# Query projections as seven products of halves, score tiles in banks of their own, block transfers over three queues

## The chip, the cores and the metric

The kernel runs on one core of a Trainium2 chip. The metric is the device time of one execution in microseconds. The kernel before took 1106.41 us, the median of three runs (1105.07 to 1107.13).

## The reference, cut to what matters

All data are float32. There are 1024 rows of width 512, 32 query heads and 8 key and value heads of width 128, so that a group of four query heads shares one key and value head.

```python
def attn(x, w_q, w_k, w_v, w_o):                # x: (1, 1024, 512), w_q: (512, 4096)
    q = (x @ w_q).reshape(B, S, Hkv, g, D)      # Hkv = 8 groups, g = 4 heads, D = 128
    k = (x @ w_k).reshape(B, S, Hkv, D)
    v = (x @ w_v).reshape(B, S, Hkv, D)
    scores = einsum("bqhgd,bkhd->bhgqk", q, k) * D ** -0.5
    scores = where(causal, scores, -inf)
    return einsum("bhgqk,bkhd->bqhgd", softmax(scores), v).reshape(B, S, -1) @ w_o

x = x + layernorm(attn(layernorm(x), w_q, w_k, w_v, w_o))
x = x + layernorm(ffn(layernorm(x)))            # a linear layer plus routed low-rank experts
```

The feed-forward part at the end is not touched by the change.

## The kernel before

The 1024 rows are 8 tiles of 128, t = 0 to 7. A *block* is one group of heads g and one tile t of queries, and there are 64. A *pair* is two tiles of one group, 256 queries (u = 0 to 3). Lines 86 to 88 fix the order: groups 0 to 5 one after the other, four pairs each, and then groups 6 and 7 in turn, pair by pair, with u = 0, 3, 2, 1. In the loop from line 798 on, block i brings together the scores of block i, the attention-weighted values of block i - 2 (line 803), the output projection of a pair finished earlier (line 808, even i), the query projection of the next pair (lines 687 to 694, odd i) and the key and value projections that fall due (lines 695 to 713). The pieces stand in a list `then`, and `run_share` deals it out: a quarter of its columns after each of the four steps of scores. The query pieces stand ahead of the rest.

**Query projection** (`project_q`, line 337). It makes the transposed queries of 4 heads x 256 rows. The contraction of 512 is four chunks of 128, so a pair takes 16 matmuls of 256 columns, a float32 matmul being two records in the trace. Two heads share a PSUM bank, and `nc.scalar.mul` (line 350) scales them and writes them to qT. The group's weights are two tiles, `wq0` for heads 0 and 1 and `wq1` for heads 2 and 3, loaded by ScalarE's queue for a new group (line 722) in its predecessor's block t = 6.

**Scores** (`scores`, line 404). A block has four steps j. A step takes 32 queries of each of the 4 heads, 128 rows, against all keys up to n = 128 t + 32 (j + 1): one or two matmuls of at most 512 columns. VectorE adds the mask (line 426) and takes the maximum (428), Pool writes zeroes into the rest of p (431), ScalarE takes the exponential and its sum (433). A step later VectorE takes the reciprocal (439), ScalarE scales p (440), and VectorE transposes p in 32 x 32 pieces into T (446). The score tile is two banks, and two of them exist. Where t is below 4, a score fits into one bank, and the step of an odd j takes the second bank of the tile of the step before it (lines 410 to 414).

**Block transfers** (`to_keys`, line 458). After the last step of a block, 16 DMAs bring T into the layout K that the values' matmuls read, queries becoming columns. Blocks 3 to 62 issue all of them on SP's queue; the first three and the last issue in turn on SP, SP and Pool (lines 452 to 454). T and K have one buffer for even and one for odd t.

**Banks.** PSUM has eight: four in the two score tiles, one for the weighted values (`bank_pv`), three for all else (`bank`).

**Order on the engines.** Matmuls, transposes, DMAs and the instructions under `keep` stay in the order of the program. The framework may place the others, the Pool's sums of weights among them, and adds semaphores where data demand them. VectorE, ScalarE and Pool each work through their queue in order. Pool also holds `combine_o` (line 500), four subtractions per group for an output projection that is already made of seven products of halves (`project_o_pair`, line 514).

Of the kernel before, what the change touches and what calls it, by code (L numbers as in the profile page):

```python
# [22 lines left out]
def kernel(  # L23
# [28 lines left out]

    nc = tc.nc
    S, H = x.shape
    D = P
# [30 lines left out]
    blocks = [(g, 2 * u + e) for g, u in pairs for e in range(2)]  # L88
    N = len(blocks)
    N2 = (G - 2) * NT  # L90

    def keep(ins):
        return tc.keep_in_program_order(ins)
# [26 lines left out]
    def load_q(g, i, by=nc.scalar):  # L120

        if weights.get(("q", i), (None,))[0] == g:
            return
        hw = R * D // 2
        w = wp.tile([P, KC, hw], F32, tag=f"wq{i}", name=f"wq_{g}_{i}", bufs=1)
        load(w, w_q[:, ts(2 * g + i, hw)].rearrange("(c p) n -> p c n", p=P), by)
        weights["q", i] = (g, w)

    def load_v(gv, i, by=nc.scalar):

# [111 lines left out]
    def bank(name):  # L242
        return ps_m.tile([P, 512], F32, tag="pm", name=name)
# [81 lines left out]
    def project_k(g, qb):  # L325
        def finish(pm):
            kT = kTs[g, qb] = act.tile([P, QB], F32, tag="kT", name=f"kT_{g}_{qb}", bufs=2 * NQB)
            nc.scalar.copy(kT, pm)

        def term(c):  # L330
            return weights["k", g][:, c, :], xnT[qb][:, c, :]

        return chained(
            lambda: bank(f"pk_{g}_{qb}"), [lambda c=c: term(c) for c in range(KC)], finish
        )

    def project_q(g, u):

        pm = {}

        def get(j):
            if j % 2 == 0:
                pm[0] = bank(f"pq_{g}_{u}_{j}")
            return pm[0][:, ts(j % 2, PQ)]

        def finish(j):
            if j == 0:
                qTs[g, u] = act.tile([P, PQ // SQ, R, SQ], F32, tag="qT", name=f"qT_{g}_{u}")
            if j % 2:
                nc.scalar.mul(  # L350
                    qTs[g, u][:, :, j - 1 : j + 1, :].rearrange("p s h q -> p h s q"),
                    pm[0].rearrange("p (h s q) -> p h s q", h=2, q=SQ),
                    scale,
                )

        def term(j, c):
            w = weights["q", j // 2]
            assert w[0] == g
            rhs = xnT[u * PQ // QB][:, c, ts(u % (QB // PQ), PQ)]
            return w[1][:, c, ts(j % 2, D)], rhs  # L360

        work = []
        for j in range(R):
            terms = [lambda j=j, c=c: term(j, c) for c in range(KC)]
            if j == 0:
                ends = lambda pm: finish(0)
            else:
                ends = lambda pm, j=j: finish(j)
            work += chained(lambda j=j: get(j), terms, ends, PQ)
        return work  # L370

    turned, keyed = {}, {}

# [30 lines left out]
    def scores(g, t, j):  # L404

        n = t * P + (j + 1) * SQ
        full = (t + 1) * P
        name = f"{g}_{t}_{j}"

        if t < TPB and j % 2:  # L410
            s = score_tile.pop(0)[:, QB:]
        else:
            s = ps_s.tile([P, S], F32, tag="s", name=f"s_{name}")
            score_tile[0] = s
        for c0 in range(0, n, QB):
            w = min(QB, n - c0)
            matmul(
                s[:, c0 : c0 + w],
                qTs[g, t // 2][:, (t % 2) * NSUB + j, :, :].rearrange("p h q -> p (h q)"),
                kTs[g, c0 // QB][:, :w],  # L420
                start=True,
                stop=True,
            )
        pin = keep if blocks.index((g, t)) >= N2 + 2 else lambda ins: ins
        rescale_scores()
        keep(nc.vector.tensor_tensor(s[:, n - SQ : n], s[:, n - SQ : n], smask, ALU.add))  # L426
        nmax = small.tile([P, 1], F32, tag="nmax", name=f"nmax_{name}")
        keep(nc.vector.tensor_reduce(nmax, s[:, :n], AX.X, ALU.max, negate=True))  # L428
        p = act.tile([P, S], F32, tag="p", name=f"p_{name}", bufs=3)
        if n < full:  # L430
            nc.gpsimd.memset(p[:, n:full], 0.0)  # L431
        total = small.tile([P, 1], F32, tag="total", name=f"total_{name}")
        keep(nc.scalar.activation(p[:, :n], s[:, :n], AF.Exp, bias=nmax, accum_out=total))  # L433
        finish_scores()
        work_off(1 + len(deferred) // 5)

        def rescale():
            rec = small.tile([P, 1], F32, tag="rec", name=f"rec_{name}")
            keep(nc.vector.reciprocal(rec, total))  # L439
            keep(nc.scalar.mul(p[:, :n], p[:, :n], rec))  # L440

        def finish():
            if j == 0:
                turned[g, t] = turn_view(turn_tile("T", g, t), t)
            pin(
                nc.vector.transpose(  # L446
                    turned[g, t][:, :, j, :, :].rearrange("p b k q -> p k b q"),
                    p[:, :full].rearrange("p (k b q) -> p k b q", b=R, q=SQ),
                )
            )  # L450
            if j == NSUB - 1:
                three = (nc.sync, nc.sync, nc.gpsimd)
                alone = 3 <= blocks.index((g, t)) < N - 1
                to_keys(g, t, by=three[:1] if alone else three)

        score_tile["rescale"], score_tile["finish"] = rescale, finish

    def to_keys(g, t, by=(nc.sync,)):

        src = turned.pop((g, t))  # L460
        dst = keyed[g, t] = turn_view(turn_tile("K", g, t), t)
        for h in range(R):
            for b in range(NSUB):
                load(dst[ts(b, SQ), h], src[ts(h, SQ), b], by[(h * NSUB + b) % len(by)])
# [217 lines left out]
    def projections(i):  # L682
# [5 lines left out]
        if i == 0:  # L688
            later["q"] = project_q(*pairs[m])
            q = later["q"][: 2 * KC]  # L690
        elif i == 1:
            q = later["q"][2 * KC :]
        elif i % 2 and m < len(pairs):
            q = project_q(*pairs[m])
        if i < N2:
            if t == 2:
                other += project_k(g, 1)
# [56 lines left out]
    def weave(a, b):  # L754

        na, nb = sum(c for c, _ in a), sum(c for c, _ in b)
        merged, at, bt, b = [], 0, 0, list(b)
        for c, f in a:
            merged.append((c, f))
            at += c  # L760
            while b and (bt + b[0][0] / 2) * na <= at * nb:
                bt += b[0][0]
                merged.append(b.pop(0))
        return merged + b
# [33 lines left out]
    for i in range(N):  # L798
# [13 lines left out]
            begins = ffn_router(t)  # L812

        rest = o + weave(o_pair, other + pv[:2] + begins[1:] + pv[2:])
        then = begins[:1] + q + ends[:-1] + rest[:4] + ends[-1:] + rest[4:]
        for n in range(NSUB):
            scores(*blocks[i], n)
            run_share(then, n, NSUB)
        if i == 1:
            combine_o(0)  # L820
        if i == NT:
# [68 lines left out]
```

## Time and profile before

| what | us |
|---|---|
| median of 3 runs | 1106.41 |
| the profiled execution's own time | 1105.28 |
| its span | 1103.5 |
| TensorE busy | 1074.5 |
| VectorE busy | 654.0 |
| ScalarE busy | 491.2 |
| Pool busy | 113.8 |
| query projections, 1024 matmul records | 235.7 |
| scores, 768 matmul records | 273.8 |
| weighted values, 576 matmul records | 277.3 |

A line of the profile that describes a group of instructions has the source line, the engine and operation, the tile written and the tiles read, the shape and the count, then the busy time in us, the mean duration of one in ns, and the engine's idle time ahead of it with what ended that. A line of waits has the engine and line that waited, what it waited for, the total in us, the number of waits and the longest. A row of stretches has, for each engine, the busy time and the number of instructions, then TensorE's granted clock and the share and rate of the DMA engines. The durations of single matmuls overlap, so the distance between their starts tells their cost, not the duration.

### The profile page before, as it was taken

How to read it: one execution, taken by the hardware profiler on the slowest of the kernel's cores; microseconds unless marked ns; L12 is line 12 of the kernel's file. 1: busy time of each engine (PE TensorE's matmuls, PEld its weight loads, DVE VectorE, ACT ScalarE, POOL GpSimd, SP SyncE). 2: the span in 40 equal slices, each digit the busy share in tenths (PEclk: the TensorE clock that was granted, in tenths of full speed). 3: DMA queues.
4: the chain of work that ended last, by engine and by line, in shares of the span. 5: the costliest groups of instructions: out<-in, count | busy, mean ns of one | idle time of the engine just before them, and what ended most of it. 6: DMA issues, size and time to landing. Idle time of an engine off the chain costs nothing.

```text
span 1103.5 us, 12827 instructions
## 1 busy us (share of the span) xinstructions
PE 1074.5 (97%) x3836; PEld 704.5 (64%) x3836; DVE 654.0 (59%) x1529; ACT 491.2 (45%) x991; POOL 113.8 (10%) x299
## 2 busy tenths in 40 slices
PE   8899999999999999999999999999999999999895
PEld 6676666666776666656676666666777556466452
DVE  4466555765465545766456654765446766566746
ACT  2554534554354434554354443555335554453501
POOL 2400012000020002000020000100020110111212
PEclk9999999999999999999999999999999999999998
DMA  5145342455125431454224441365333655444221
GB/s 181 40 107 141 67 115 58 125 144 115 24 68 155 107 82 45 113 144 105 52 60 125 121 104 37 93 176 123 86 102 100 166 144 116 127 107 104 68 67 38
DMA packets 79061, 111.82 MB, mean 101 GB/s; under 512 B 18176, under 2 KB 50560, under 8 KB 78992
## 3 DMA queue, kind: packets, MB, share of 16 engines
q1 hardware_dynamic: 52976, 82.08, 31.5%
q10 hardware_dynamic: 25040, 27.27, 7.9%
q0 software_dynamic: 976, 1.65, 0.6%
q8 instruction: 31, 0.51, 0.2%
q14 instruction: 38, 0.31, 0.1%
HBM read 33.34 MB, written 2.10 MB: 32 GB/s over the span
## 4 chain that ended last, share of the span: by engine, by line
PE 82%; DVE 7%; ACT 5%; DMA 2%; issue 1%; SPq 1%; POOL 1%; ACTq 0%; POOLq 0%; DVEq 0%
PE po L100 20%; PE s L100 18%; PE pq L100 16%; PE pk L100 4%; PE pv L100 4%; PE pe L100 4%; PE pa L100 3%; ACT p L433 2%; PE pO L100 2%; PE pc L100 2%; PE pb L100 2%; PE pd L100 2%; DVE T L446 2%; PE pf L100 2%; DVE nmax L428 2%; ACT p L440 2%
## 5 line engine op out<-in xcount | busy, mean ns | idle before, releaser
L100 PE MATMUL s<-kT,qT 128*128 128x512 f32 (+15 forms) x768 | 273.8, 465 | 8.7 <-ACT p L433 8.6
L100 PE MATMUL po<-K,v 128*128 128x512 f32 x576 | 277.3, 596 | 4.3 <-DMA K<-T 2.6
L433 ACT ACTIVATE p<-s,nmax 128x32 f32<-128x32 f32 (+31 forms) x256 | 179.2, 700 | 203.1 <-DVE nmax L428 197.9
L440 ACT ACTIVATE p<-p,rec 128x32 f32<-128x32 f32 (+31 forms) x256 | 187.9, 734 | 179.3 <-DVE rec L439 121.0
L446 DVE STREAM_TRANSPOSE T<-p 128x128 f32<-128x128 f32 (+7 forms) x256 | 198.2, 775 | 100.4 <-ACT p L440 89.4
L100 PE MATMUL pq<-xnT,wq 128*128 128x256 f32 x1024 | 235.7, 379 | 0.0
L100 PEld LDWEIGHTS s<-kT,qT 128*128 128x128 f32 x768 | 144.0, 190 | 137.4 <-issue 105.5
L100 PEld LDWEIGHTS pq<-xnT,wq 128*128 128x128 f32 x1024 | 192.8, 190 | 38.5 <-issue 16.5
L428 DVE TENSOR_REDUCE nmax<-s 128x1 f32<-128x32 f32 (+31 forms) x256 | 180.6, 705 | 8.2
L100 PEld LDWEIGHTS po<-K,v 128*128 128x128 f32 x576 | 107.8, 191 | 78.0 <-issue 63.3
L426 DVE TENSOR_TENSOR s<-s,smask 128x32 f32<-128x32 f32 x256 | 47.8, 187 | 132.2 <-PE s L100 131.5
L431 POOL MEMSET p<- 128x96 f32 (+2 forms) x192 | 29.7, 155 | 848.4 <-DVE T L446 782.9
L439 DVE RECIPROCAL rec<-total 128x1 f32<-128x1 f32 x256 | 39.8, 155 | 55.1 <-ACT p L433 53.2
L100 PE MATMUL pv<-wv,xnT 128*128 128x256 f32 x256 | 69.1, 388 | 0.9 <-ACT xnT L264 0.9
L350 ACT ACTIVATE qT<-pq 128x512 f32<-128x512 f32 x64 | 38.1, 595 | 71.1 <-PE pq L100 71.1
L474 ACT COPY attnT<-po 128x512 f32<-128x512 f32 x64 | 37.4, 584 | 63.2 <-PE po L100 63.0
L100 PE MATMUL pk<-xnT,wk 128*128 128x512 f32 x128 | 64.5, 593 | 0.0
L100 PE MATMUL pa<-wo,attnT 128*128 128x256 f32 x224 | 62.7, 390 | 0.0
L100 PEld LDWEIGHTS pv<-wv,xnT 128*128 128x128 f32 x256 | 49.1, 194 | 11.0 <-issue 2.7
L100 PEld LDWEIGHTS pa<-wo,attnT 128*128 128x128 f32 x224 | 41.6, 192 | 19.4 <-issue 14.5
L433 ACT ACTIVATION_READ_ACCUMULATOR p<-s,nmax 128x1 f32 x256 | 49.5, 193 | 0.0
L523 DVE TENSOR_TENSOR sums<-attnT 128x256 f32<-128x256 f32 x28 | 11.9, 425 | 56.8 <-ACT attnT L474 56.7
(120 smaller groups left out, 776.6 us busy)
## 6 DMA issues: line engine op xcount, KB each, us to landing
K<-T SPq DMA_DIRECT2D x128, 128.0 KB, 2.4
K<-T SPq DMA_DIRECT2D x128, 112.0 KB, 2.2
wq<-in_w_q_dram ACTq DMA_DIRECT2D x27, 512.0 KB, 4.8
K<-T SPq DMA_DIRECT2D x128, 96.0 KB, 2.2
K<-T SPq DMA_DIRECT2D x128, 80.0 KB, 2.1
K<-T SPq DMA_DIRECT2D x123, 64.0 KB, 2.0
wo<-in_w_o_dram ACTq DMA_DIRECT2D x28, 256.0 KB, 3.8
K<-T SPq DMA_DIRECT2D x123, 48.0 KB, 1.9
```

What stands on the lines that cost most here:

```text
L100: keep(nc.tensor.matmul(*args, **kw))
L350: nc.scalar.mul(qTs[g, u][:, :, j - 1 : j + 1, :].rearrange("p s h q -> p h s q"), pm[0].rearrange("p (h s q) -> p h s q", h=2, q=SQ), scale,)
L426: keep(nc.vector.tensor_tensor(s[:, n - SQ : n], s[:, n - SQ : n], smask, ALU.add))
L428: keep(nc.vector.tensor_reduce(nmax, s[:, :n], AX.X, ALU.max, negate=True))
L431: nc.gpsimd.memset(p[:, n:full], 0.0)
L433: keep(nc.scalar.activation(p[:, :n], s[:, :n], AF.Exp, bias=nmax, accum_out=total))
L439: keep(nc.vector.reciprocal(rec, total))
L440: keep(nc.scalar.mul(p[:, :n], p[:, :n], rec))
L446: nc.vector.transpose(turned[g, t][:, :, j, :, :].rearrange("p b k q -> p k b q"), p[:, :full].rearrange("p (k b q) -> p k b q", b=R, q=SQ),)
L474: nc.scalar.copy(o, po)
L523: nc.vector.tensor_tensor(s1, a21, a22, ALU.add)
```

## The change

For pairs 2 to 24 of 32 (`QW`), the 4 heads x 512 inputs of weights and the 512 inputs x 256 rows are each cut into 2 x 2 blocks, and the product of the two is made of seven products of such blocks with sums before and after them:

- `combine_x`, for each pair, in the even block ahead: four Pool subtractions of 128 x 256.
- `combine_q`, once for each group, in the even block ahead of its first such pair: four Pool operations of 128 x 512 on the weights. One overwrites half of `wq1`.
- `project_q_halves`: 28 matmuls of 128 columns in four banks, two products to a bank. Each writes four runs of 32 columns. `merge` then adds the products into qT: one ScalarE copy that writes both of two places and seven VectorE adds of 128 x 256.
- In odd blocks with t above 1, these query pieces are woven with the first three fifths of the rest. In blocks with t = 1, they stay ahead of it.

The scale moves from the queries to the keys, at the same number of instructions. The score of every step takes a tile of its own. The transfers of every block are issued on SP, SP and Pool in turn.

```diff
+    QW = range(2, N2 // 2 + 1)
...
+    def combine_q(m):
+        g = pairs[m][0]
+        if weights.get("sq", (None,))[0] == g:
+            return
+        w = [weights["q", i][1] for i in range(2)]
+        hk = KC // 2
+        a11, a12, a21, a22 = w[0][:, :hk], w[0][:, hk:], w[1][:, :hk], w[1][:, hk:]
+        s1, s2, s4 = (
+            ffn.tile([P, hk, 2 * D], F32, tag="hy", name=f"sq_{g}_{n}", bufs=3) for n in range(3)
+        )
+        for dst, p, q, op in (
+            (s1, a21, a22, ALU.add),
+            (s2, s1, a11, ALU.subtract),
+            (a21, a11, a21, ALU.subtract),
+            (s4, a12, s2, ALU.subtract),
+        ):
+            keep(nc.gpsimd.tensor_tensor(dst, p, q, op))
+        weights["sq", 0] = (a11, a12, s4, a22, s1, s2, a21)
+        weights["sq"] = (g,)
+
+    def combine_x(m):
+        u = pairs[m][1]
+        hk = KC // 2
+        xp = xnT[u * PQ // QB][:, :, ts(u % (QB // PQ), PQ)]
+        b11, b12, b21, b22 = xp[:, :hk, :P], xp[:, :hk, P:], xp[:, hk:, :P], xp[:, hk:, P:]
+        t12, t34 = (ffn.tile([P, 2, hk, P], F32, tag="x", name=f"tx_{m}_{n}") for n in range(2))
+        t1, t2, t3, t4 = t12[:, 0], t12[:, 1], t34[:, 0], t34[:, 1]
+        for dst, p, q in ((t1, b12, b11), (t2, b22, t1), (t3, b22, b12), (t4, b21, t2)):
+            nc.gpsimd.tensor_tensor(dst, p, q, ALU.subtract)
+        weights["tx"] = (b11, b21, b22, t4, t1, t2, t3)
...
-            nc.scalar.copy(kT, pm)
+            nc.scalar.mul(kT, pm, scale)
...
-                nc.scalar.mul(
+                nc.scalar.copy(
...
-                    scale,
...
+    def project_q_halves(m):
+        g, u = pairs[m]
+        hk = KC // 2
+        pm = {}
+
+        def half(e, h):
+            return both(e)[:, h]
+
+        def both(e):
+            q = qTs[g, u][:, ts(e, NSUB), :, :]
+            return q.rearrange("p s (x h) q -> p x s (h q)", x=2)
+
+        def add(dst, src, to):
+            nc.vector.tensor_tensor(dst, src, to, ALU.add)
+
+        def merge(b):
+            one, two = pm[b][:, 0], pm[b][:, 1]
+            if b == 0:
+                nc.scalar.copy(both(0), one.unsqueeze(1).to_broadcast([P, 2, NSUB, 2 * SQ]))
+                add(half(0, 0), two, half(0, 0))
+            elif b == 1:
+                add(half(1, 0), one, half(0, 1))
+                add(half(0, 1), two, half(1, 0))
+            elif b == 2:
+                add(half(1, 1), one, half(0, 1))
+                add(half(1, 0), one, half(1, 0))
+                add(half(1, 0), two, half(1, 0))
+            else:
+                add(half(0, 1), one, half(0, 1))
+
+        order = (0, 1, 5, 6, 4, 2, 3)
+
+        def piece(n, c, k):
+            i, b, x = order[n], n // 2, n % 2
...
+            if x == c == k == 0:
+                whole = bank(f"pq_{g}_{u}_{b}")
+                pm[b] = whole.rearrange("p (x s n) -> p x s n", x=2, s=NSUB)
...
+            matmul(
+                pm[b][:, x, :, ts(c, SQ)],
+                weights["sq", 0][i][:, k, ts(c, D)],
+                weights["tx"][i][:, k, :].rearrange("p (s q) -> p s q", q=SQ),
+                start=(k == 0),
+                stop=(k == hk - 1),
+            )
+            if c == 1 and k == hk - 1 and (x == 1 or n == 6):
+                merge(b)
...
-        if t < TPB and j % 2:
-            s = score_tile.pop(0)[:, QB:]
-        else:
-            s = ps_s.tile([P, S], F32, tag="s", name=f"s_{name}")
-            score_tile[0] = s
+        s = ps_s.tile([P, S], F32, tag="s", name=f"s_{name}")
...
-                three = (nc.sync, nc.sync, nc.gpsimd)
-                alone = 3 <= blocks.index((g, t)) < N - 1
-                to_keys(g, t, by=three[:1] if alone else three)
+                to_keys(g, t)
...
-    def to_keys(g, t, by=(nc.sync,)):
+    def to_keys(g, t, by=(nc.sync, nc.sync, nc.gpsimd)):
...
-            q = project_q(*pairs[m])
+            q = project_q_halves(m) if m in QW else project_q(*pairs[m])
...
+        if i % 2 and i // 2 + 1 in QW and blocks[i][1] > 1:
+            cut = len(rest) * 3 // 5
+            q, rest = weave(q, rest[:cut]), rest[cut:]
         then = begins[:1] + q + ends[:-1] + rest[:4] + ends[-1:] + rest[4:]
         for n in range(NSUB):
             scores(*blocks[i], n)
             run_share(then, n, NSUB)
+            if i % 2 == 0 and n < 2 and i // 2 + 1 in QW:
+                (combine_x, combine_q)[n](i // 2 + 1)
```

More of the change, by code (lines that the diff above doesn't have):

```diff
@@ L370, in project_q @@
         return work
+    def project_q_halves(m):
[26 more added lines that the diff above has]
+            i, b, x = order[n], n // 2, n % 2
+            if n == c == k == 0:
+                qTs[g, u] = act.tile([P, PQ // SQ, R, SQ], F32, tag="qT", name=f"qT_{g}_{u}")
+            if x == c == k == 0:
+                whole = bank(f"pq_{g}_{u}_{b}")
+                pm[b] = whole.rearrange("p (x s n) -> p x s n", x=2, s=NSUB)
+            assert weights["sq"] == (g,)
+            matmul(
[7 more added lines that the diff above has]
+                merge(b)
+        return [
+            (P, lambda n=n, c=c, k=k: piece(n, c, k))
+            for n in range(7)
+            for c in range(2)
+            for k in range(hk)
+        ]
     turned, keyed = {}, {}
```

## The prediction, made before the run

> **What bounds the kernel now.** I read the page first, then the stretches of one group, then the matmul groups by shape, then the waits, then the chain at the end. The page:
>
> ```profile
> PE 1074.5 (97%) x3836; PEld 704.5 (64%) x3836; DVE 654.0 (59%) x1529; ACT 491.2 (45%) x991; POOL 113.8 (10%) x299
> ...
> PEclk9999999999999999999999999999999999999998
> ```
>
> TensorE is busy in 97% of the span at full clock, but the ends of matmuls are modelled, so I count starts. A 256-column record (a float32 matmul is two records) starts 216 ns before the next when nothing is in the way, a 512-column one 429 ns. Adding that for all 3836 records, 111 ns for those of 128 columns or less, gives 1059.5 us. What the starts lie further apart than that sums to 36.2 us: 11 before 58 us, 13 from there to 1034 (7.6 of them at scores), 12 in the last stretch. So the middle is bound by the number of columns that TensorE streams. The eight blocks of group 3 (t = 0 to 7), one row each:
>
> ```profile
> core 0: us, PE busy (x) PEld busy (x) DVE busy (x) ACT busy (x) POOL busy (x), PEclk, DMA share, GB/s
> 391.70:405.80 14.10, 13.42 (x51) 8.69 (x50) 8.68 (x26) 5.30 (x15) 0.46 (x3) 1.00 0.46 102
> 405.80:421.00 15.20, 15.20 (x57) 10.47 (x56) 4.58 (x17) 5.32 (x15) 0.45 (x3) 1.00 0.28 62
> 421.00:434.40 13.40, 12.86 (x47) 8.65 (x46) 9.40 (x24) 6.00 (x15) 0.45 (x3) 1.00 0.14 33
> 434.40:446.80 12.40, 12.04 (x46) 8.29 (x46) 6.86 (x17) 6.67 (x14) 5.48 (x7) 1.00 0.34 85
> 446.80:459.70 12.90, 12.90 (x51) 8.85 (x50) 11.18 (x24) 6.61 (x14) 0.30 (x2) 1.00 0.30 71
> 459.70:474.90 15.20, 15.20 (x57) 10.49 (x57) 9.24 (x18) 8.11 (x15) 0.60 (x4) 1.00 0.64 170
> 474.90:494.40 19.50, 19.50 (x64) 11.80 (x63) 14.18 (x26) 10.09 (x16) 0.46 (x3) 1.00 0.62 164
> 494.40:513.00 18.60, 18.60 (x62) 11.40 (x61) 10.51 (x17) 10.66 (x15) 0.46 (x3) 1.00 0.45 100
> ```
>
> See two things: t = 4 has VectorE busy in 11.18 of 12.90 us (87%) and TensorE still never idle; and the odd blocks, where the query projections stand, leave VectorE the most room.
>
> The waits that TensorE does have, and one of them (t = 2, second score tile) in order of time:
>
> ```profile
> PE s L100 <- ACT p L433: 8.6, 17, 1.2
> PE po L100 <- DMA K<-T: 2.6, 1, 2.6
> ```
>
> ```profile
> 424.56 0.19 ACT L433 ACTIVATION_READ_ACCUMULATOR p<-s,nmax 128x1 f32 x1
> ...
> 424.80 0.81 PE L100 MATMUL s<-kT,qT 128*128 128x320 f32 x2 [0.54 <-ACT p L433]
> ```
>
> The score of an odd j starts when the exponential of the j before it, in the other half of the same tile, has ended (424.56 + 0.19 = 424.75). All these waits are at odd j with t below 4. By starts, with the 50 to 100 ns that the next weight load adds, they cost 4.9 us in the first group, 7.6 in groups 1 to 5 and 1.0 in the last block, which I leave alone.
>
> The end, from the chain:
>
> ```profile
> 1045.65 0.59 SPq L106
> 1046.28 1.91 DMA K<-T
> 1048.38 1.33 PE po L100 x2
> ```
>
> The last transfer but one block leaves SP in 16 issues 0.63 us apart (10.1 us), and TensorE waits 2.6 us for it; the starts after it lie 211 ns further apart than in the middle, some 1.7 us more.
>
> **What the Trainium skill says.** "TensorE: Matmul & The Clock Gate", section Back-to-back issue gap: in a stream of weight loads and matmuls both set the spacing, and at small N the load counts (N=128: about 81 ns per matmul where the matmul alone would take 56). That is the question here, as every new matmul has new weights and 128 columns. The trace answers nearly: scores of 128 columns start 109 ns and 111 to 112 ns before what follows, and eight records of 143 columns with eight different weights follow at 122 ns:
>
> ```profile
> 897.89 1.14 PE L100 MATMUL pl<-ra_sb,hT 128*128 128x143 f32 x8
> ...
> 898.87 1.45 PE L100 MATMUL po<-K,v 128*128 128x512 f32 x3
> ```
>
> (0.98 us for eight; 143 against 128 columns accounts for 12 ns.) "PSUM — Partial Sum Buffer", Specifications: cachelines are 8 bytes, and non-contiguous access slows matmuls. The new outputs are four runs of 32 elements; no matmul of this trace writes such a pattern. "SBUF — State Buffer", Who interferes with whom: VectorE instructions with two SBUF inputs, or in a two-port mode, contend with GpSimd; one SBUF input doesn't. The trace agrees for the first: a 15-element scale at 1045.50 took 0.85 us beside Pool's 1.27 us subtraction, 0.22 us at 1058.0. The new adds read PSUM and one SBUF operand. "DMA: Bandwidth & Descriptors", Issuing engines are not separate DMA queues: another issuing engine saves only issue time. The trace has 0.63 us per issue on SP and 0.50 on Pool.
>
> **The change, part by part.**
>
> *Products.* A pair has 16 matmuls of 256 columns, 32 records x 216 = 6.91 us; it gets 28 of 128 columns, 56 records. At 111 ns that is 6.22 us, 0.69 less, for 23 pairs 15.9 us, all on TensorE's path. Bounds: 109 ns (18.5 us) and 122 ns, the 143-column row, for a weight load or output pattern that is in the way (1.7 us). I take 111, the two-in-a-row scores.
>
> *Merges.* Seven adds of 128x256 from PSUM per pair. 128x768 takes 944 ns and 128x512 687 (L547), so 256 elements cost 257 and an add 430 ns: 3.0 us per pair, 69 us on VectorE. ScalarE has one 595 ns copy in place of two: 14 us less. All of it falls in odd blocks. In group 3, t = 3 VectorE goes from 6.86 to 9.9 us while the block falls from 12.4 to about 11.0 (0.7 from products, 0.6 from the score waits): 90%; t = 5 to 12.2 of 14.5 (84%), t = 7 to 13.5 of 17.9. In even-numbered groups, which also project v, it is lower. The order on VectorE is fixed: an add that waits for its product holds the mask, maximum and transpose behind it, and so the next exponential and the score after that. A bank must be merged before the second bank after it may start, when the v projection takes no third one. With b1's 16 records (1.8 us) as cover, the ScalarE copy and the add (0.6 + 0.43 and some 0.4 for semaphores and the ends of matmuls) just fit if neither queue is busy. I charge 1 us for t = 3 in the three odd-numbered groups, 0.3 us for six blocks t = 1 (not woven), nothing for the others, where a score (0.8 to 1.7 us) stands between: 5 us. Bounds 0 and 16 (0.7 us per pair). Below nothing isn't possible: no merge removes a wait.
>
> *Pool's sums.* 4 subtractions of 128x256 per pair and 4 of 128x512 for each of 7 groups. 128x512 takes 1.27 us (L509), so half is 0.64 to 0.72: 2.7 us per pair and 5.1 per group, some 98 us on an engine that has 114. They run when the products of the pair before have ended, in the rest of the odd block (2 to 5 us), and for a new group behind the landing of wq (median 4.8 us) in block 6, a block of 19.5 us ahead of its use. Behind them in Pool's queue stand the zeroes of p (L431), which the exponential waits for, and Pool's share of the transfers. Steady state: nothing, covered by block 6 and the rest of odd blocks; without that cover 2.7 us per pair. In the first group there is no cover: in block 2 Pool has combine_x and combine_q on top of combine_o (5.1 us), so the zeroes of its third score tile and the transfers of block 1 come about 4 us later. I let that eat the 4.9 us of score waits there and 0.5 more. Bounds: -3 and +3.
>
> *Transfers.* 60 blocks get 11 issues on SP (7.0 us) and 5 on Pool (2.5) for 16 on SP (10.1). In the middle they are hidden both before and after: attended two blocks later. 300 issues of 0.5 us add 150 us to Pool, which ends near 360 of 1090 us. At the end 3.1 us come off ahead of the 2.6 us wait and the 1.7 us after it: -3.5. Bounds -4.5 and -1, as what follows may wait for the last block instead.
>
> *Own banks.* A score waits for the exponential two before it, as t above 3 does, where there is no wait. Of 7.6 us in groups 1 to 5 I take 6.5. Bounds 3 and 7.6.
>
> Sum: -15.9 + 5 + 0.5 - 3.5 - 6.5 = -20.4. The profiled execution took 1105.3 us (span 1103.5), so 1084.9; it lies 1.1 below the median of the three runs, so I forecast 1086.
>
> **The rivals.**
>
> *Late merges.* The in-order adds cost about 0.7 us per pair, 16 in place of 5: 1097, and up to 1106 where the score waits return as well. For it: 90% of VectorE in t = 3, directly ahead of t = 4 at 87%. Against: t = 4 itself, with no wait.
>
> *All hidden.* No merge waits, the first group gains 3: 1105.3 - 15.9 - 3 - 4.5 - 7.6 and 1.1, 1075; with the 109 ns record less still.
>
> *VectorE sets the blocks (slower).* Half of the 3.0 us of adds ends up on the path in each pair, because score, transpose and merge queue behind one another: 34.5 us in place of 5, 1115. It is slower from a stall of 1.1 us per pair on. Against it speaks the room in t = 1 and 7 (30% and 57% busy before).
>
> *The record is dear (slower).* If weights or the 32-element runs hold the spacing at 150 ns, a pair costs 8.4 us, 1.5 more: 34 us in place of -15.9, 1136. Break-even is near 127 ns. The 143-column row speaks against it, nothing shows the output pattern.
>
> That the change doesn't do what it says is not open: in the order of instructions the 23 pairs have the new matmuls and adds.
>
> **Chances.** Forecast 50%; all hidden 15%; late merges 22%, of which 3 within 0.2% of before; VectorE sets the blocks 8%; dear record 5%. Within 0.2% (2.2 us) is what a measurement here can't tell from no change. Faster 84%, same 3%, slower 13%. The range, 1075 to 1101, leaves out the two slower cases, the worst of the late merges and a few per cent below.
>
> **What would show it.** pq records of 128 columns spaced 109 to 112 ns, 56 for each of 23 pairs; VectorE's adds near 430 ns; no score at odd j held by the exponential just before it; the wait for K near the end gone; VectorE at 85 to 90% in t = 3 of groups 3 and 5 with at most 1 us of idle TensorE. It is wrong if the spacing is above 122 ns, or if pq matmuls wait for VectorE or Pool in sum more than some 10 us.

## The result, and the profile after

The changed kernel takes 1091.32 us, the median of four runs (1088.93 to 1092.57); the kernel before took 1105.74 beside it (four runs, 1104.09 to 1107.13). The ratio is 0.9868, with a 95% interval from 0.9845 to 0.9890: 14.4 us faster, where the forecast had 20.4 us. The profiled execution took 1091.45 us with a span of 1089.7.

The page of the kernel after: its engines, the granted clock, and three groups of instructions:

```profile
PE 1057.3 (97%) x4388; PEld 711.0 (65%) x4388; DVE 705.2 (65%) x1690; ACT 480.6 (44%) x968; POOL 360.0 (33%) x719
...
PEclk9999999999999999999999999999999999999998
...
L108 POOL DMA_DIRECT2D K<-T x320 | 158.2, 501 | 262.4 <-DVE s L518 57.3
...
L423 DVE TENSOR_TENSOR qT<-pq,qT 128x256 f32<-128x256 f32 x161 | 63.3, 413 | 36.0 <-ACT qT L429 28.1
...
L162 POOL TENSOR_TENSOR tx<-xnT 128x256 f32<-128x256 f32 x46 | 33.4, 727 | 89.8 <-PE pq L102 80.3
```

The sizes are those that were estimated: 7 adds of products into qT for each of 23 pairs at 413 ns (430 expected), Pool's subtractions of 128x256 at 0.73 us, 320 transfers at 0.50 us, and 360 us of work on Pool. The new matmuls in order of time:

```profile
153.02 1.06 PE L102 MATMUL pq<-xnT,sq 128*128 128x128 f32 x8
...
153.92 1.06 PE L102 MATMUL pq<-tx,wq 128*128 128x128 f32 x8
```

Eight records from start to start take 0.90 us, 112 ns each. Over all 128-column products the mean is 111.4, waits left out. So 56 records of a pair cost 6.24 us where 32 records of 256 columns (216 ns each) cost 6.91, and 23 pairs 15.5 us less, against 15.9 predicted. The slowing by output that is not contiguous, which the prediction weighed, doesn't show: plain 128-column records are spaced 109 to 112 ns.

Group 3 again, t = 0 to 5:

```profile
core 0: us, PE busy (x) PEld busy (x) DVE busy (x) ACT busy (x) POOL busy (x), PEclk, DMA share, GB/s
387.40:400.35 12.95, 12.95 (x51) 8.88 (x50) 8.59 (x25) 4.34 (x13) 2.76 (x7) 1.00 0.50 124
400.35:414.88 14.53, 14.53 (x81) 10.65 (x80) 6.80 (x25) 4.94 (x14) 5.79 (x13) 1.00 0.24 54
414.88:427.50 12.62, 12.62 (x48) 8.76 (x47) 9.28 (x24) 6.05 (x15) 2.94 (x8) 1.00 0.17 42
427.50:439.40 11.90, 11.22 (x69) 8.32 (x67) 8.85 (x24) 6.97 (x15) 10.48 (x15) 1.00 0.36 90
439.40:452.45 13.05, 13.02 (x50) 8.98 (x51) 11.48 (x25) 6.33 (x12) 3.04 (x10) 1.00 0.32 81
452.45:467.30 14.85, 14.69 (x81) 10.47 (x80) 11.55 (x24) 8.36 (x17) 5.72 (x13) 1.00 0.54 160
```

Now see t = 3, the fourth row: VectorE is at 74% (90% was expected), TensorE idles 0.7 us, and Pool is busy for 10.48 of 11.90 us.

What TensorE waits for after the change, and what ends the program (groups of its last line, the first of them from the kernel before):

```profile
PE s L102 <- ACT p L525: 4.7, 2, 3.4
PE s L102 <- DVE qT L423: 2.8, 4, 2.3
PE po L102 <- ACT p L525: 2.3, 1, 2.3
PE s L102 <- ACT attnT L564: 2.1, 3, 0.7
PE po L102 <- DMA K<-T: 1.3, 1, 1.3
```

```profile
L886 POOLq DRAIN  x3: 46/102/2797, 1098.4 to 1103.2; - x3
...
L982 POOLq DRAIN  x3: 46/102/7534, 1081.4 to 1089.4; - x3
L982 SPq DRAIN  x3: 7/7/7, 1085.4 to 1089.2; - x3
```

Seventeen waits of scores for exponentials have become two, and one of these is long. Pool's closing drain takes 7.53 us (2.80 before), while the last store of the result has landed at 1085.3. Two names need care. The three waits for attnT are the scores after t = 3 of groups 1, 3 and 5; these scores don't read attnT, but they read qT, and in group 3 a sum of qT ended at 439.29 and the copy to attnT at 439.38, just ahead of the score's weights at 439.40. The wait of values for p, 2.3 us, is the one near the end: the last transfer of their K landed at 1032.20, and a wait of TensorE on DMAs came through at 1032.23. So it is the wait for K that the prediction wanted gone, 2.6 us before.

The ledger by stretches of blocks, from each block's first score to the next one's; in brackets what the matmuls' starts lie further apart than their columns need, here called loss (none is given ahead of block 0):

| stretch | before | after | difference |
|---|---|---|---|
| ahead of block 0 | 26.31 | 27.83 | +1.52 |
| blocks 0 to 2 | 24.67 (4.66) | 20.16 (0.17) | -4.51 |
| block 3 | 12.11 (0.37) | 15.07 (3.99) | +2.96 |
| blocks 4 to 7 | 73.18 (0.25) | 71.96 (0.33) | -1.22 |
| group 1 | 122.26 (3.90) | 122.45 (6.77) | +0.19 |
| groups 2 and 4 | 266.30 (1.94) | 259.86 (0.86) | -6.44 |
| groups 3 and 5 | 242.57 (5.86) | 234.82 (3.39) | -7.75 |
| blocks 48 to 62 | 267.16 (0.94) | 267.13 (0.94) | -0.03 |
| block 63 and the end | 68.94 (12.06) | 70.43 (10.30) | +1.49 |

The sum is -13.8. The stretch ahead of block 0 runs the same instructions in both; TensorE's slow start there lasted longer in this execution (128-column records are still 213 ns apart at 14 us; before, they are 109 apart from 11.5 us on). In the runs below it takes 25.0 to 27.8 us, so a single span is good to about 1.5 us. Four stretches lack what the forecast gave them: block 3, group 1, the end, and to a small part groups 3 and 5.

Not all of a loss is a wait. After some long waits the granted clock was 0.5 for a while, and the starts lay about twice as far apart. This row of the kernel after is the stretch that follows the wait of block 9:

```profile
157.81:161.22 3.41, 2.86 (x5) 1.70 (x6) 2.78 (x12) 2.42 (x8) 2.62 (x6) 0.50 0.20 42
```

Records of 512 columns start 854 ns apart there, against 429. Of the 5.06 us that block 9 loses, the wait is 3.4 and these slow starts are 1.5. Block 3, with waits of 1.3 and 2.3 us, has no such stretch; which waits bring one stays open.

### The profile page after: what moved, and what is told of

It reads as the page before. It is cut to its first block, busy times and chain, and to the rows that moved or that the text cites. A ratio compares the mean times of both kernels' runs of the same rounds, so it can differ in the third digit from the quotient of the medians.

```text
span 1089.7 us, 15062 instructions
## 1 busy us (share of the span) xinstructions
PE 1057.3 (97%) x4388; PEld 711.0 (65%) x4388; DVE 705.2 (65%) x1690; ACT 480.6 (44%) x968; POOL 360.0 (33%) x719
## 4 chain that ended last, share of the span: by engine, by line
PE 89%; DVE 4%; POOL 2%; DMA 2%; ACT 1%; issue 1%; POOLq 0%; ACTq 0%; DVEq 0%
PE po L102 21%; PE s L102 20%; PE pq L102 17%; PE pv L102 5%; PE pk L102 5%; PE pa L102 4%; PE pe L102 4%; PE pO L102 2%; PE pc L102 2%; PE pb L102 2%; PE pd L102 2%; PE pf L102 2%; DMA emap_i<-in_expert_map_dram 1%; POOL K L108 1%; DVE nmax L520 1%
## 5 line engine op out<-in xcount | busy, mean ns | idle before, releaser
L102 PE MATMUL po<-K,v 128*128 128x512 f32 x576 | 280.3, 595 | 3.9 <-ACT p L525 2.3
L108 POOL DMA_DIRECT2D K<-T x320 | 158.2, 501 | 262.4 <-DVE s L518 57.3
L102 PE MATMUL pq<-xnT,wq 128*128 128x128 f32 (+1 forms) x656 | 113.8, 321 | 0.0
L102 PEld LDWEIGHTS pq<-xnT,wq 128*128 128x128 f32 x656 | 100.6, 191 | 14.7 <-issue 7.7
L423 DVE TENSOR_TENSOR qT<-pq,qT 128x256 f32<-128x256 f32 x161 | 63.3, 413 | 36.0 <-ACT qT L429 28.1
L102 PE MATMUL pv<-wv,xnT 128*128 128x256 f32 x256 | 73.0, 390 | 0.7 <-ACT xnT L300 0.7
L162 POOL TENSOR_TENSOR tx<-xnT 128x256 f32<-128x256 f32 x46 | 33.4, 727 | 89.8 <-PE pq L102 80.3
L102 PEld LDWEIGHTS pq<-tx,wq 128*128 128x128 f32 x368 | 49.6, 192 | 9.1 <-issue 7.7
L102 PEld LDWEIGHTS pq<-tx,sq 128*128 128x128 f32 x368 | 49.6, 192 | 8.2 <-issue 7.9
L102 PE MATMUL pq<-tx,sq 128*128 128x128 f32 x368 | 53.6, 275 | 0.0
```

What stands on the lines that cost most here:

```text
L102: keep(nc.tensor.matmul(*args, **kw))
L108: keep(by.dma_start(dst, src))
L162: nc.gpsimd.tensor_tensor(dst, p, q, ALU.subtract)
L423: nc.vector.tensor_tensor(dst, src, to, ALU.add)
```

## Experiments

My theory at this point: products and banks gave what was forecast, and what is missing went into side effects of the transfers on Pool, namely the drain and the landing of the expert map. The rival: VectorE's sums, or two score tiles in flight in place of four. Neither held in this form.

### Each part alone

The kernel before with the three queues only (e1):

```diff
-                alone = 3 <= blocks.index((g, t)) < N - 1
-                to_keys(g, t, by=three[:1] if alone else three)
+                to_keys(g, t, by=three)
```

> The kernel before with one part of the change alone: every block's sixteen transfers go over SP, SP and Pool in turn. My theory after the result (transfers on Pool cost time at their side effects): slower than before by 2 to 6 us, of which 3 to 5 us is a longer closing drain of Pool (2.8 us before, 7.5 us after) and 1 to 3 us a later landing of the expert map, which is the last of six loads on Pool's queue; 1107 to 1112 us. The prediction's own reckoning of this part: faster by 1 to 4.5 us, 1101 to 1105 us.

1111.85 us, ratio 1.0044 (1.0032 to 1.0056): slower by 4.9, as my theory said. In its ledger group 1 is 4.1 us longer and the end 1.0 (the loss is 2.3 smaller; the drain is 4.7 longer, and 3.2 of that reach the end); the rest stands as before, within 0.5. So on the old kernel the transfers were indeed hidden in the middle, and spreading them gained nothing there.

The kernel before with banks of its own for every score only (e2):

```diff
-        if t < TPB and j % 2:
-            s = score_tile.pop(0)[:, QB:]
-        else:
-            s = ps_s.tile([P, S], F32, tag="s", name=f"s_{name}")
-            score_tile[0] = s
+        s = ps_s.tile([P, S], F32, tag="s", name=f"s_{name}")
```

> The kernel before with one part alone: every score tile has its own banks. My theory: the waits of scores for each other in groups 1 to 5 (6.6 to 7.6 us) and in block 2 (4.9 us) go, less what two tiles in flight in place of four cost in the last block (1.4 us): faster by 6 to 10 us, 1096 to 1100 us. Rival (the banks give less than forecast, since other waits move up, and this is where the missing 6 us lie): faster by 2 to 4 us, 1102 to 1104 us.

1095.37 us, ratio 0.9895 (0.9878 to 0.9913): faster by 11.6, more than expected. Blocks 0 to 2 give 4.5 us and groups 1 to 5 8.2. The last block takes 3.3 back, most of it in one wait and what follows it:

```profile
PE po L100 <- DMA K<-T: 4.9, 1, 4.9
```

Before, this wait was 2.6. The granted clock was 0.5 for 6.8 us after it, where it was 3.4 us before, which is another 1.0 us. With a bank of its own a score comes out in another order against the feed-forward's work on VectorE; the last transpose of the last block but one now stands behind a layer norm's statistics that wait 1.3 us for Pool, and SP's first transfer for it is issued 4.7 us into block 63 where it was 2.3.

The changed kernel without the three queues and the own banks, which leaves the seven products, their sums and the weave (e3):

```diff
-        s = ps_s.tile([P, S], F32, tag="s", name=f"s_{name}")
...
+        if t < TPB and j % 2:
+            s = score_tile.pop(0)[:, QB:]
+        else:
+            s = ps_s.tile([P, S], F32, tag="s", name=f"s_{name}")
+            score_tile[0] = s
...
-                to_keys(g, t)
+                three = (nc.sync, nc.sync, nc.gpsimd)
+                alone = 3 <= blocks.index((g, t)) < N - 1
+                to_keys(g, t, by=three[:1] if alone else three)
```

> The kernel before with one part alone: seven products of halves for 23 pairs with their sums and the weave; block transfers and score tiles as before. My theory: 15.9 us less of TensorE's stream, 1 to 4 us of it given back in waits for the merges: faster by 12 to 15 us, 1091 to 1094 us. Rival (late merges or Pool's sums swallow what the ledger of the whole change lacks): faster by 8 to 10 us only, 1096 to 1098 us.

1104.20 us, ratio 0.9980 (0.9966 to 0.9995): 2.2 us, where 12 to 15 were expected and even the rival had 8. The stream is 15.5 us shorter, but the profiled span only 2.9: waits and slow starts took back 12.6. The part with the surest gain gives nearly nothing by itself. Of its waits, TensorE's alone, the second is new:

```profile
PE s L102 <- ACT p L530: 10.0, 19, 1.2
PE po L102 <- DMA wo<-in_w_o_dram: 6.3, 3, 2.7
```

The longest, 2.7 us at t = 5 of group 1, was followed by 3.4 us at a granted clock of 0.5.

The changed kernel with the transfers as before (e4):

```diff
-                to_keys(g, t)
+                three = (nc.sync, nc.sync, nc.gpsimd)
+                alone = 3 <= blocks.index((g, t)) < N - 1
+                to_keys(g, t, by=three[:1] if alone else three)
```

> The changed kernel with the third part undone: the transfers of all blocks but the first three and the last go by SP alone, as before. My theory: Pool's closing drain falls from 7.5 to about 3 us and the expert map lands earlier, so the time is 5 to 8 us under the changed kernel: 1083 to 1087 us. Rival (the shortfall lies in merges and in two score tiles in flight, and earlier transfers helped as forecast): the same as the changed kernel or up to 3 us above it, 1091 to 1094 us.

1093.10 us, ratio 0.9881 (0.9867 to 0.9896), which can't be told from the changed kernel; 5 to 8 us less were expected. So my theory falls as the whole story: the drain is back at 2.80 us and block 9 loses 0.86 in place of 5.06, and yet nothing is gained. In groups 1, 3 and 5 the block t = 5 now loses 2.1, 2.1 and 1.5 us (0.35 each after the change), block 4 loses 1.6 more (the granted clock was 0.5 there from 60.9 to 64.3 us, after waits in block 3), and the end takes 72.5 us. The three queues cost 4.9 us on the old kernel and pay for themselves on the new one. The wait at t = 5 of group 1, in order of time:

```profile
204.17 0.30 PEld L102 LDWEIGHTS po<-K,v 128*128 128x128 f32 x2 [1.70 <-ACT p L525]
204.20 1.10 PE L102 MATMUL po<-K,v 128*128 128x512 f32 x2 [1.54 <-DMA wo<-in_w_o_dram]
```

The view names the load of wo, which the values don't read. The landings settle it: the last of K's sixteen transfers was issued at 200.06 and landed at 203.745, the first of TensorE's waits on DMAs came through at 203.77, and the values started at 204.20 after the rest of these waits in turn. Two of the four loads of wo landed only at 204.57 and 205.51, when the values were under way. TensorE waits for K. That transfer took 3.7 us, where one issued at 196.05 took 2.0: the loads of wo (256 KB each, issued from 199.2 on) were under way beside it. The Trainium skill, "DMA: Bandwidth & Descriptors", Issuing engines are not separate DMA queues, says that transfers of all issuing engines interleave on the same DMA engines; this pair of numbers agrees.

Why does it wait now, and not before? From the start of that block (t = 5, group 1), by the trace:

| run | K's last transfer lands | first matmul of the values starts |
|---|---|---|
| before | 5.2 | 10.5 |
| the change, SP only | 3.9 | 4.4, after its wait |
| after | 1.4 ahead of it | 2.7 |
| the change, SP only, no weave (below) | 4.0 | 9.8 |

K is no later than it was. The weave deals the products out among the first part of the block's other work, so the values no longer stand behind all of them; they are reached 7 us sooner.

### The weave and the map

The expert map is a load of 7.5 KB for the feed-forward, the last of six on Pool's queue after block 8 begins. Here it is moved ahead of the others and to SP (e5):

```diff
+        load(emap_i, expert_map.partition_broadcast(P))
         load(ra_sb[:, :, :NR], router_wt...
...
-        load(emap_i, expert_map.partition_broadcast(P), nc.gpsimd)
```

> The changed kernel with one load moved: the expert map goes first of the six loads, and over SP's queue, not last on Pool's. Theory (the 5.1 us lost in block 9 come from the map's late landing, behind K_7's transfers on Pool): block 9 loses under 1 us, group 1 is 4 us shorter, the whole 3.5 to 4.5 us faster than the changed kernel, 1087 us. Rival (block 9 waits for the transposes and sums whatever the map does): no change, 1091 us.

1092.58 us, ratio 0.9885 (0.9865 to 0.9906): no change, and block 9 loses 6.40. By itself this would speak for the rival. But SP's queue was no better a place: it holds K_7's other transfers, and the map was issued 14.6 us into block 8 where Pool had it at 11.6. It landed later still. So this run decides nothing; the map is loaded much earlier in a run below.

As e4 (transfers by SP), without the weave (e6):

```diff
-        if i % 2 and i // 2 + 1 in QW and blocks[i][1] > 1:
-            cut = len(rest) * 3 // 5
-            q, rest = weave(q, rest[:cut]), rest[cut:]
```

> The changed kernel with transfers by SP alone (as in the run of that name) and without the weave: the 56 records of the products come first in their block, and the block's other work, the weighted values among it, after them. New theory (the weave brings the weighted values of blocks t=5 forward to a place where SP's sixteen transfers, 10 us after the last transpose, have not landed): the waits for K at t=5 of groups 1, 3 and 5 (1.7 us each[...]) go, 5 us less; sums at t=3 end earlier, up to 3 us less; 1085 to 1088 us against 1093 of the woven one. Rival (K is late there because the blocks became shorter, not because of the order): the waits stay and the time is 1092 to 1094 us; or the products in one go wait for VectorE's sums, and it is slower, 1095 to 1100 us.

1085.87 us, ratio 0.9824 (0.9803 to 0.9845): the expected value. The loss at t = 5 is 0.00 in all three groups, at t = 3 it falls from 0.87 to 0.00, and in block 3 from 4.00 to 1.54. Of the waits of values for a DMA one is left, the one at the end:

```profile
PE po L102 <- DMA K<-T: 4.9, 1, 4.9
```

What the weave was worth shows too: t = 7 of groups 0, 2 and 4 loses 0.58 us each without it.

The changed kernel, three queues and all, without the weave (the same three lines taken out, e7):

> The changed kernel, three queues and all, without the weave. If the weave is what makes three queues needed, then without it they bring nothing in the groups: this kernel stands 1 to 4 us above the run with SP alone and no weave in blocks 0 to 62, for the map's late landing, and the end is shorter by 5.6 us of waits and longer by 3.3 us of Pool's drain; 1086 to 1090 us. Rival (the weave hides VectorE's sums, as the prediction had it): 1093 to 1098 us.

1086.24 us, ratio 0.9827 (0.9804 to 0.9850), about 4.5 us under the changed kernel by the ratios. Waits for sums of qT come to 1.7 us in its list (1.0 of them at t = 7 of groups 0, 2 and 4), fewer than with the weave. Against e6, blocks 3 to 62 differ by the map (group 1 longer by 3.7) and by 1.1 us in groups 3 and 5, where t = 4 has K a little earlier; the end is 2.0 us shorter. Without the weave the three queues are again worth nothing on balance.

The map loaded well ahead, in the changed kernel (e9):

```diff
-        load(emap_i, expert_map.partition_broadcast(P), nc.gpsimd)
...
+        if i == 4:
+            load(emap_i, expert_map.partition_broadcast(P))
         if i == NT:
             prepare_ffn()
```

> The changed kernel with one load moved well ahead: the expert map is loaded by SP at block 4, long before its use after block 8. (In the run that put it on SP's queue after block 8 it was issued 14.6 us into block 8, later than the 11.6 us of the changed kernel, since SP's queue held K_7's transfers too, and block 9 lost 6.4 us.) Theory: the landing of the map sets block 9's wait; block 9 loses under 0.5 us in place of 5.06, 4 to 5 us less in all: 1087 us. Rival (Pool's differences or VectorE's load are what holds the sums in block 9): 1090 to 1092 us.

1087.44 us, ratio 0.9836 (0.9821 to 0.9850). Block 9 loses 0.53 in place of 5.06 and group 1 is 4.5 us shorter. In these runs the loss of block 9 goes with the landing of the map, counted from the start of block 8:

| run | landed | block 9 loses |
|---|---|---|
| products alone | 14.4 | 0.27 |
| banks alone | 16.4 | 0.00 |
| before | 16.7 | 0.98 |
| the change, SP only | 16.6 | 0.86 |
| three queues alone | 19.1 | 5.07 |
| after | 20.1 | 5.06 |
| the change, map on SP's queue | 20.7 | 6.40 |
| the change, map loaded at block 4 | long before | 0.53 |

The landing doesn't decide alone. A map at 16.4 costs nothing with own banks only, while e10 below (16.5) and e6 (16.9), without the weave, lose 1.6 and 1.2. From 19 us on every kernel loses 5 us or more, the two not listed too (e7 19.5, e8 20.4; 5.2 each). All of these have a stretch at a granted clock of 0.5 after the wait.

How a load of 7.5 KB holds TensorE is seen in the changed kernel in order of time:

```profile
155.06 0.72 POOL L162 TENSOR_TENSOR tx<-xnT 128x256 f32<-128x256 f32 x1 [0.25 <-PE pq L102]
155.18 0.63 DVE L244 CAST emap_f<-emap_i 128x15 f32<-128x15 int32 x1 [1.97 <-DMA emap_i<-in_expert_map_dram]
...
155.84 1.17 DVE L247 TENSOR_SCALAR mexp<-emap_f 128x15 f32<-128x15 f32 x8
...
157.01 0.17 DVE L518 TENSOR_TENSOR s<-s,smask 128x32 f32<-128x32 f32 x1
...
158.36 0.74 PE L102 MATMUL s<-kT,qT 128*128 128x224 f32 x1 [3.39 <-ACT p L525]
```

VectorE stands at the cast until 155.18, then spends 1.8 us on nine operations of 15 elements, and only then reaches the mask of a score whose matmuls started at 148.0. The score that waits needs the bank of that one. The Trainium skill, "SBUF — State Buffer", Who interferes with whom, counts a cast among the operations that can take the port pair shared with Pool; beside Pool's subtraction this one took 0.63 us, in the kernel before, with Pool idle, 0.17. The same load in the kernel before and after, the lines on the issue and on its landing:

```profile
L106 POOL DMA_DIRECT2D emap_i<-in_expert_map_dram x1: 535/535/535, 145.4 to 145.4; - x1
...
DMA to landing us min/median/max: 7.5/7.5/7.5
```

```profile
L108 POOL DMA_DIRECT2D emap_i<-in_expert_map_dram x1: 537/537/537, 146.6 to 146.6; - x1
...
DMA to landing us min/median/max: 8.5/8.5/8.5
```

It is issued 1.2 us later though its block began 1.2 us earlier, behind K_7's five transfers on Pool, and takes 1 us longer.

The seven products alone once more, as in e3, but without the weave (e10):

> The seven products alone, as in the run of that part (transfers and score tiles as before), but without the weave. Theory (the weave took away what the products gave, by bringing values forward of their K): the waits for K at t=5 of groups 1, 3 and 5 go (4.9, 2.4 and 2.3 us of loss) and t=3 ends up to 1 us earlier each; 1093 to 1097 us against 1104.2 of the woven one. Rival (shared score tiles are what the products run into): 1102 to 1105 us.

1093.63 us, ratio 0.9894 (0.9880 to 0.9907), against 0.9980 with the weave: 11.7 us faster than before by the ratio, in place of 2.2. This is the plainest measure: the products with their sums were worth about what was forecast (10.4 us, if the prediction's terms for products, merges and Pool's sums are added), and the weave took most of it away while SP alone moved the blocks. The DMA waits of 6.3 us are gone from its list, which begins

```profile
PE s L102 <- ACT p L530: 11.4, 19, 1.4
PE po L102 <- DMA K<-T: 2.6, 1, 2.6
```

### Parts chosen

A first choice from the ledger (e8): products from the third pair on, shared score tiles kept for the last four blocks, three queues for the first three blocks, t = 3 of groups 1, 3 and 5 and the last three; the map first, by SP.

```diff
-    QW = range(2, N2 // 2 + 1)
+    QW = range(3, N2 // 2 + 1)
...
+        last = blocks.index((g, t)) >= N - 4
+        if last and j % 2:
+            s = score_tile.pop(0)[:, QB:]
...
-                to_keys(g, t)
+                i = blocks.index((g, t))
+                some = i < 3 or i >= N - 3 or (i < N2 and g % 2 and t == 3)
+                to_keys(g, t, by=(nc.sync, nc.sync, nc.gpsimd) if some else (nc.sync,))
```

> The changed kernel with each part only where the ledger says that it pays: products from the third pair on (22 of 32); own banks but for the last four blocks; three queues for the first three blocks, the t=3 blocks of groups 1, 3 and 5 and the last three; the expert map first, by SP. Worked out from the spans: the run with SP alone 1091.0, start luck +1.3, blocks 3 and 4 -5.0, t=5 in three groups -4.7, block 9 -0.7, last block from 72.5 to 66 -6.5; sum 1075.4 of span, 1077 us. If one of the readings is wrong its term stays: 1079 to 1084 us. Rival (waits only move): 1086 to 1090 us.

1085.05 us, ratio 0.9816 (0.9794 to 0.9838), 8 above the sum I had worked out. The map on SP's queue is the mistake of e5 again (block 9 loses 5.17). Block 3 went from 15.07 to 11.84, but blocks 2 and 4 gave 1.6 back. The end came to 67.2. Pool issued 50 transfers here, and its drain lies between the two that were known:

```profile
L990 POOLq DRAIN  x3: 46/102/4759, 1078.0 to 1083.3; - x3
```

The second choice (e11): products for 23 pairs, the weave only at t = 5 and 7 of groups 0, 2 and 4, the map at block 4, three queues for the first three blocks and the last two, shared score tiles for the last four.

```diff
-        if i % 2 and i // 2 + 1 in QW and blocks[i][1] > 1:
+        if i % 2 and i // 2 + 1 in QW and blocks[i][0] % 2 == 0 and blocks[i][1] > 3:
```

> Products for 23 pairs; the weave only for blocks t=5 and t=7 of groups 0, 2 and 4; own banks but for the last four blocks; three queues for the first three blocks and the last two; the map loaded at block 4. From the run with SP alone and no weave, span 1083.4: block 9 -1.0, blocks 7, 23 and 39 -0.6 each, the last block from 72.5 to 66.9 -5.6; 1075.1 of span, 1077 us. Pool issues 31 transfers in all, and its closing drain is expected at 3.2 us (2.80 for 26, 4.76 for 50). Rival (waits move again): 1081 to 1085 us.

1078.66 us (five runs, 1078.18 to 1080.12), ratio 0.9762 (0.9749 to 0.9775): by the ratios 12 us faster than the changed kernel, and 26 faster than before. Group 1 takes 116.6 us, block 3 12.6, the end 68.0 (66.9 expected; a score waits 2.8 us there). Pool's drain is 3.12 us with 30 transfers.

| run | parts | ratio to before |
|---|---|---|
| e1 | three queues | 1.0044 |
| e2 | banks | 0.9895 |
| e3 | products, weave | 0.9980 |
| e10 | products | 0.9894 |
| e4 | products, weave, banks | 0.9881 |
| e6 | products, banks | 0.9824 |
| after | products, weave, banks, three queues | 0.9868 |
| e7 | products, banks, three queues | 0.9827 |
| e9 | after, map at block 4 | 0.9836 |
| e11 | chosen parts | 0.9762 |

## Why the prediction was right or wrong

The direction and the range held; the forecast was 5 us too low, with the term of the products nearly exact and errors of both signs in the others. Its nearness is in part luck: blocks 0 to 2 came out 5.0 us better than their term, the end 5.0 us worse, and the map's 4.1 us had no term.

*Products.* Right: -15.5 us of stream for -15.9, at 111.4 ns a record for 111.

*Merges.* Charged at 5 us. Of the places, t = 3 of the groups 1, 3 and 5 was right (0.87 us each for 1 expected) and t = 1 wrong (none in groups 3 and 5). Block 3, at no charge, had 2.4 us of waits for sums, and t = 5 of groups 1, 3 and 5 had 0.35 each. These places sum to some 6 us (2.4 + 2.6 + 1.05), so that the 5 us charged were near the sum by luck: more than half of it fell where nothing was charged. The failed step is "nothing for the others, where a score (0.8 to 1.7 us) stands between". It charges the blocks that aren't woven and treats the weave as harmless, with nothing put down for what it does to the rest of the block. The weave moves the sums to the end of the block, next to the score that needs them, and the values to its front. Without it, t = 3 and t = 5 of these groups lose nothing (e6, e7, e10). By the ratios it costs 4.5 us in the changed kernel (after against e7), and 9.5 where SP moves the blocks and score tiles are shared (e3 against e10).

*Transfers.* "In the middle they are hidden both before and after: attended two blocks later." True without the weave, whether SP issues alone or not (e1, e6, e7). With it and SP alone it is false: e4 loses 5.7 us at t = 5, and 1.05 with three queues. In the change as it was made it fails in block 3 only, where the values wait 1.3 us for K. I had compared the sixteen issues with the length of two blocks, but a block's start isn't where the values stand; their place in the block decides, and the change moves it.

*The end.* Forecast -3.5, measured +1.5. The mechanism was there: against SP alone, three queues cut the loss of the end by 5.3 us (e4 and after, 72.5 to 70.4 although 3.2 us more of the drain reach the end). The wait for K that was to be gone is still 2.3 us. Two terms were missing. Own banks, for which the forecast looked at groups 1 to 5 only, add 3.3 to the last block (e2). And 300 more transfers on Pool lengthen its closing drain from 2.80 to 7.53 us, of which 3.2 reach the end of the program. The trace of before can't show the drain's dependence on a count, only that Pool ends with one.

*Pool's sums and queue.* "Steady state: nothing" held. What failed is that I listed behind Pool's queue the zeroes and the transfers, and not the six loads that `prepare_ffn` puts on the same queue once. The last of them is awaited by VectorE in a fixed order. That is +4.1 us in block 9, and it was in reach: the wait was in the trace of before (0.98 us, with VectorE standing at the same cast), but I had counted it among the scores' waits for each other. At that landing own banks do remove it (e2); at the later one they don't.

*Own banks and the first group.* Forecast -6.5 in groups 1 to 5; alone they give 8.2 there. In blocks 0 to 2 the 4.5 us of score waits came off in full, where the forecast let Pool's sums eat them and 0.5 more. Pool's work may hold TensorE, but one block later and for less: of the 3.99 us that block 3 loses, 1.5 are the values' wait for K. Its last transfer landed at 53.98, one of five on Pool that left from 49.2 us on, behind Pool's sums; SP's last landed at 53.77, so that Pool alone isn't shown to be the cause. The other 2.4 are the sums of qT. Without the weave the values come later, no wait for K is left, and 1.54 us of loss stay, 0.9 of them for sums (e6).

*The rivals.* None of the four was what happened. The sums cost about what the forecast allowed them, the records were not dear, and VectorE was busy for at most 88% of a block in group 3.

What stays open: how much of the 1.5 us ahead of block 0 is chance (the spread over the runs would allow all of it), which waits are followed by a lower clock, and how the drain's length goes between 50 and 325 transfers. The ledgers and clocks are of one profiled execution of each kernel; the ratios rest on four or more.

## What to carry to other kernels

When a change reorders a block, write down for each consumer where in the block it now stands, and compare that with when its data land; a transfer that is hidden by "two blocks" may be hidden only by the old order. After a long wait, read the granted clock of the stretch that follows: what the wait costs can be half as much again. Parts of one change aren't additive: three queues cost 4.9 us alone, and were the repair for a wait that another part had made. And when an engine's queue gets new work, list everything that is ever issued on it, the loads that happen once included, and who waits for each in a fixed order.

## What the runs showed of the hardware

- Pool's drain at the end of the program took 2.80 us with 26 transfers issued by Pool in the whole run, 3.12 with 30, 4.76 with 50, 7.45 with 325 and 7.53 with 326, the same to within 5 ns in all runs of one count. The first three lie on a line of 0.08 us per transfer. The last two differ by 0.08 us as well, but lie far below that line.
- A 128-column float32 product with new weights each time, written as four runs of 32 elements, is spaced 111.4 ns from the next; plain ones are spaced 109 to 112.
- A 64 KB transfer of a block issued while four 256 KB loads ran took 3.7 us to land, where it took 2.0 without them.
- After a wait of 3.4 us TensorE's granted clock was 0.5 for 3.4 us, and 512-column records started 854 ns apart in place of 429 (block 9 after the change). After the 4.9 us wait of e2 near its end it was 0.5 for 6.8 us.
